# Kept padded buffers and 576-byte rows in the expert choice, and the sampling's preparation by halves of the image

## The chip, the cores and the metric

The kernel runs on one core of a Trainium2 chip. The metric is the time of one launch on the device, in microseconds (us). The core has five engines, each with its own queue of instructions: PE (matrix products; its weight loads are shown as PEld), DVE and ACT (vector and activation work), POOL (here mostly indirect loads, which it issues itself) and SP (which only issues transfers). Transfers are carried out by 16 DMA engines.

## The reference

Four blocks of a network on x of shape (4, 128, 64, 64): in each, x gains a "conv" of its layer norm over channels, and then a "ffn" of the layer norm of its tokens. The kinds differ by layer: involution and a recurrence; deformable sampling and expert choice; a clipped convolution and expert choice; attention and a top-2 mixture. The change lies in layer 0's recurrence, layer 1's sampling and the two expert choices:

```python
# sampling (x has been normalized over channels)
off = conv2d(x, w_off, b_off)                      # 9 taps x (dy, dx)
mask = sigmoid(conv2d(x, w_mod, b_mod))
py = row + ky + dy;  px = column + kx + dx
y0 = floor(py);  x0 = floor(px);  ly = py - y0;  lx = px - x0
# v00 v01 v10 v11: the pixels at (y0 | y0+1, x0 | x0+1), 0 outside the image
sampled = (v00*(1-ly)*(1-lx) + v01*(1-ly)*lx + v10*ly*(1-lx) + v11*ly*lx) * mask
out = einsum('bckhw,ock->bohw', sampled, weight) + bias

# expert choice (x has been normalized over its 128 features), E=64, K=8
probs = softmax(x @ gate_w.T + gate_b, axis=tokens)
topv, topi = top_k(probs per expert, K)
pooled = sum over k of x[topi] * topv              # per image and expert
out = gelu([pooled, 1] @ weight1); out = [out, 1] @ weight2
x[topi] += out * topv
```

## The kernel before

x stays on the chip as `xs`, 128 channels by 4 images of 4096 tokens; a chunk is 512 tokens (8 image rows, CH), so an image has 8 chunks (NCH). The phases run one after the other. The code under `manual_schedule` (ORDERED engines: the sweeps of the recurrence, the sampling's plans and loop, both phases of the expert choice) is issued in program order on every engine and queue; around it, as at the start of the recurrence, a scheduler orders the instructions of a queue. A wait of one instruction holds everything behind it on the same engine. Transfers by nc.sync go out on SP's queue in that order.

**Recurrence** (L452 to L587). It loads W, its transpose `rnn_wt`, V's transpose `rnn_vt` and gamma and beta (L473 to L480), then sums V's transpose up on PE (`rnn_pb`, L514), normalizes the tokens (L181 to L188) and sweeps over the sequence in segments; 1028 to 1236 us in the profile. Whether a further sweep is needed is decided by a flag that is read back.

**Sampling** (`deformable`, L590 on). For every image a table in HBM, `dcn_table`, holds for every (row, column) of a 66 x 66 grid four pixels of 128 channels each, the corners of a square: 2 KB, so that one indirect load fetches what one tap of a token needs. `plan(b)` is the preparation of one image, written as a generator that yields after each small step:

- 16 zero writes for the borders (L667, L669), on SP's queue;
- for the 8 chunks: centring on PE (L686), a copy into the padded image `dcn_pad` (L689, DVE), squares (L694, ACT), then variances on PE (L676), root (L700), reciprocal in four parts (L704) and scaling (L710 on PE, L715 on DVE);
- four times two chunks: 16 transposes on PE (L724), ACT copies into `dcn_xt` (L726), and four writes of 512 KB into the table, one for each corner q, in rows of 512 bytes (L731);
- twice four chunks: the offsets, 72 matmul records (L744), bias (L753), transposes (L757) and copies into `dcn_off` (L762);
- `places`: the indices `dcn_idx` (L772 to L789) and the four corner weights (L796 on).

The offsets' weights and biases, the grids of positions (iota on POOL, L638, and casts on DVE, L640) and the two padded buffers (a memset of the whole on POOL, L247) are set up ahead of plan(0), which runs alone. Then a loop over images, chunks and taps issues gathers on POOL (L816), four to a chunk and tap; ACT (L830) and DVE (L833 to L841) weight the corners, PE (L856, L857) adds and transposes them two steps later, and the convolution follows. Each step (two gathers) also takes one step of the next image's plan. Gathered tiles have 14 buffers, the weighted ones 15 each.

**Expert choice** (L911 on, run for layers 1 and 2). Two images are a pair; 2 images x 64 experts are the 128 rows of `moe_chosen`. Phase A: `stat` sums up squares of a chunk (L1008 to L1018); `scales` and `inverted` give 1/deviation (L1031, L1035); `turn_scales` transposes it (L1041); `logits` multiplies the gate's product by it (L1054 to L1068: rb, the deviations spread over the experts; pl, the product); `largest` finds the 8 largest and their places (L1087 on); `exponentials` the softmax's sum (L1101); `rows` transposes a chunk's tokens (L1076), copies them (L1078) and, on POOL, their scale (L1079) into `moe_xt`, and writes 512 rows of 129 numbers into `moe_table` (L1081); `ask` fetches the chosen rows (L1108); `pool` sums them (L1122 on). `mark` and `choose` (L972, L977) turn the logits into the weights used by the add-back. Phase B loops over 16 groups of four experts, for which 2 MB of weights each come from HBM (L985, L987), and a last part adds the results back to xs.

Of the kernel before, what the change touches and what calls it, by code (L numbers as in the profile page):

```python
# [17 lines left out]
F32 = mybir.dt.float32  # L18
# [222 lines left out]
def padded_pair(net, pool, pad, name):  # L241

    side = H + 2 * pad
    out = []
    for i in range(2):
        t = pool.tile([P, side, side], F32, name=f"{name}{i}", bufs=1)
        net.nc.gpsimd.memset(t, 0.0)  # L247
        out.append(t)
    return out
# [202 lines left out]
def recurrence(net):  # L452
# [16 lines left out]
    with ExitStack() as ctx:  # L469
        sb = ctx.enter_context(tc.tile_pool(name="rnn", bufs=1))  # L470
        yp = ctx.enter_context(tc.tile_pool(name="rnn_y", bufs=3))
# [8 lines left out]
        nc.sync.dma_start(gb[:, 1:2], ins["L0_ffn_beta"])  # L480
        xn = sb.tile([P, LEN, B, SEGS], F32, name="rnn_xn")
# [58 lines left out]

        ps = ctx.enter_context(tc.tile_pool(name="rnn_ps", bufs=2, space=PSUM))
# [44 lines left out]
        with tc.manual_schedule(engines=ORDERED):  # L586
            sweep(0, True, begin())  # L587


def deformable(net):  # L590
# [5 lines left out]

    tc, nc, ins = net.tc, net.nc, net.ins
    KK, PAD = 9, 1  # L600
    SIDE = H + 2
    NO = 3 * KK
    Q4 = 4
    BANKS = {"pt": 3, "out": 2, "pd": 1, "pv": 1}
    GATHERED = 14
    with ExitStack() as ctx:
        dram = ctx.enter_context(tc.tile_pool(name="dcn_dram", bufs=1, space=bass.MemoryType.DRAM))
        tables = [dram.tile([SIDE, SIDE, 4, P], F32, name=f"dcn_table{b}") for b in range(B)]
        one = ctx.enter_context(tc.tile_pool(name="dcn", bufs=1))
        sb = ctx.enter_context(tc.tile_pool(name="dcn_s", bufs=2))  # L610
        ps = ctx.enter_context(tc.tile_pool(name="dcn_ps", bufs=2, space=PSUM))

        woff = one.tile([P, KK, 32], F32, name="dcn_woff")
        nc.vector.memset(woff, 0.0)
        nc.sync.dma_start(woff[:, :, 0 : 2 * KK], ins["L1_conv_w_off"])
        nc.sync.dma_start(woff[:, :, 2 * KK : NO], ins["L1_conv_w_mod"])
        boff = one.tile([P, 1], F32, name="dcn_boff")
        nc.vector.memset(boff, 0.0)
        for q in range(Q4):
            nc.sync.dma_start(boff[32 * q : 32 * q + 2 * KK], ins["L1_conv_b_off"])  # L620
            nc.sync.dma_start(boff[32 * q + 2 * KK : 32 * q + NO], ins["L1_conv_b_mod"])
        wk = one.tile([P, KK, P], F32, name="dcn_wk")
        nc.sync.dma_start(wk, ins["L1_conv_weight"])
        bias = one.tile([P, 1], F32, name="dcn_bias")
        nc.sync.dma_start(bias, ins["L1_conv_bias"])
        zero = one.tile([SIDE, P], F32, name="dcn_zero")
        nc.vector.memset(zero, 0.0)

        grids = []
        for axis in range(2):  # L630
            grid = one.tile([P, NT, KK], I32, name=f"dcn_grid{axis}")
# [8 lines left out]
            nc.vector.tensor_copy(t, grid)  # L640
            grids.append(t)
# [8 lines left out]
        def plan(b):  # L650
# [13 lines left out]
            for q in range(4):  # L664
                dy, dx = divmod(q, 2)
                for r in (H, H + 1) if dy else (0, H + 1):
                    nc.sync.dma_start(tables[b][r, :, q, :], zero)  # L667
                for x in (W, W + 1) if dx else (0, W + 1):
                    nc.sync.dma_start(tables[b][1 - dy : 1 - dy + H, x, q, :], zero[0:H])  # L669

            pv = bank("pv")
            squares = []

            def variances(r):
                for q in range(4):
                    nc.tensor.matmul(  # L676
                        pv[32 * q : 32 * q + 32],
                        net.ewin[:, 31 - r : 63 - r],
                        squares[4 * r + q],
                        start=r == 0,  # L680
                        stop=r == 1,
                    )

            for c in range(NCH):
# [6 lines left out]
                if c == 4:  # L691
                    variances(0)
# [3 lines left out]
            yield  # L696
            variances(1)
            yield
            rstd = sb.tile([P, CH], F32, name="ln_rstd", tag="ln_rstd", bufs=1)
            nc.scalar.activation(rstd, pv, AF.Sqrt, bias=net.eps[1e-6])  # L700
            yield
            for i in range(4):
                part = rstd[:, i * P : (i + 1) * P]
                nc.vector.reciprocal(part, part)  # L704
                yield
            for c in range(NCH):
                rows = slice(32 * (c % 4), 32 * (c % 4) + 32)
                own = 32 * (c % 4) + c // 4
                pb = bank()
                nc.tensor.matmul(  # L710
                    pb, net.ident[rows, own : own + 1].to_broadcast([32, P]), rstd[rows], start=True, stop=True
# [5 lines left out]
            for c2 in range(NCH // 2):  # L717

                xt = sb.tile([W, 2 * ROWS, P], F32, name="dcn_xt", tag="dcn_xt")
                for r0 in range(0, 2 * ROWS, 4):  # L720
# [5 lines left out]
                    nc.scalar.copy(xt[:, r0 : r0 + 4, :], pt)  # L726
# [184 lines left out]
def expert_choice(net, layer):  # L911
# [24 lines left out]
    with ExitStack() as ctx:  # L936
# [54 lines left out]
        with (  # L991
# [147 lines left out]
            for j in range(2):  # L1139
                stat(0, j)  # L1140
# [8 lines left out]
            for j in range(2, 2 * NCH):  # L1149
                stat(0, j)  # L1150
# [822 lines left out]
```

## Time and profile before

| what | us |
|---|---|
| median of 10 runs | 8188.27 |
| lowest to highest | 8182.06 to 8193.77 |
| the profiled execution, its time | 8185.38 |
| its span | 8183.6 |

The mean granted TensorE clock in it was 0.967. The stages, in us from the start of the span:

| stage | from | to |
|---|---|---|
| involution | 0 | 1028 |
| recurrence | 1028 | 1236 |
| sampling, preparation of image 0 | 1236 | 1331 |
| sampling, gather loop | 1331 | 2796 |
| expert choice of layer 1: phase A, phase B, add-back | 2796 | 2930, 3011, 3032 |
| convolution | 3032 | 3352 |
| expert choice of layer 2 | 3352 | 3585 |
| attention and the mixture | 3585 | 8183 |

A profile line of the timeline has the start, the time to the end, the engine, the line of the kernel, the operation with its output and inputs, and in brackets how long the engine had been idle and what ended it. Lines of equal operations that follow each other closely are joined, with their count behind the x. SPq is SP's queue, on which a transfer is issued; the time shown there is that of issuing (a queue that is full makes it longer), not of the transfer.

### The profile page before, as it was taken

Reading aid. Unit: us, or ns where it says so; the run is one execution under the profiler, and the core shown is the slowest. Engines: PE = TensorE matmul, PEld = TensorE weight load, DVE = VectorE, ACT = ScalarE, POOL = GpSimd, SP = SyncE. Lnnn points to the kernel's source line nnn. Section 1 sums busy time; section 2 is a strip of 40 time slices with the busy share of each in tenths; the row PEclk is TensorE's granted clock in tenths of the full one; section 3 lists DMA queues with packets and bytes.
Section 4 is the critical chain, followed back from the end, with each engine's and each line's share of the span. In section 5 each row is a group of like instructions: output and inputs, shape, how many; then the busy total and the mean of one; then the engine's idle time right before and its main releaser. Section 6 shows DMA issues by size and latency. Waiting matters only on the chain.

```text
span 8183.6 us, 144876 instructions
## 1 busy us (share of the span) xinstructions
PE 7547.4 (92%) x59022; PEld 3229.0 (39%) x59022; DVE 5535.6 (68%) x8689; ACT 3769.0 (46%) x7100; POOL 5296.2 (65%) x3019
## 2 busy tenths in 40 slices
PE   8999986777777779879999999999999999999899
PEld 2222243555555434333444344443444334444333
DVE  7888856888888642247776667766777677677155
ACT  4444433444444420313555555555555555555521
POOL 5898904777777410105888788887788777888700
PEclk9999998999999989988999999999999999999999
DMA  6434206877877570232554444544545444455400
GB/s 183 95 75 97 49 2 157 249 220 237 240 217 209 164 214 0 47 145 64 105 111 105 102 106 101 112 105 101 107 102 110 105 101 106 107 105 110 99 22 24
DMA packets 333940, 963.78 MB, mean 118 GB/s; under 512 B 43412, under 2 KB 148948, under 8 KB 275412
## 3 DMA queue, kind: packets, MB, share of 16 engines
q0 software_dynamic: 143872, 673.30, 34.9%
q1 hardware_dynamic: 189396, 281.18, 12.6%
q8 instruction: 464, 7.60, 0.4%
q14 instruction: 208, 1.70, 0.1%
HBM read 468.89 MB, written 82.78 MB: 67 GB/s over the span
## 4 chain that ended last, share of the span: by engine, by line
PE 60%; DVE 11%; DMA 8%; issue 3%; ACT 1%; POOL 1%; SPq 1%; DVEq 0%; POOLq 0%; ACTq 0%
PE att_pv L1576 15%; PE att_sc L1663 13%; PE att_mx L1520 11%; DMA dcn_g<-dcn_table,dcn_idx 6%; PE att_sc L1564 5%; DVE dcn_part L836 3%; PE conv_po L1330 3%; DVE dcn_part L833 3%; PE top_po L1876 3%; DVE dcn_sum L841 2%; DMA moe_w<-in_L_ffn_weight 1%; PE top_pw L1852 1%; DVE att_most L1531 1%; PE moe_pd L1008 1%; SPq L731 1%
## 5 line engine op out<-in xcount | busy, mean ns | idle before, releaser
L1595 POOL TENSOR_TENSOR att_acc<-att_acc,att_ex 128x2048 f32<-128x2048 f32 x640 | 2902.5, 4535 | 637.4 <-ACT att_ex L1664 618.1
L1531 DVE TENSOR_REDUCE att_most<-att_mx 128x2 f32<-128x1024 f32 x2016 | 2462.4, 1222 | 1071.0 <-PE att_mx L1520 991.5
L1664 ACT ACTIVATE att_ex<-att_sc 128x512 f32<-128x512 f32 x4096 | 2223.7, 594 | 1771.2 <-PE att_sc L1663 1488.1
L1663 PE MATMUL att_sc<-att_q,att_k 32*128 32x512 f32 x8192 | 2455.3, 606 | 0.0
L1520 PE MATMUL att_mx<-att_k,att_q 32*128 32x512 f32 x8064 | 2291.8, 647 | 13.0 <-DVE att_parts L1543 10.9
L1564 PE MATMUL att_sc<-att_rows,att_ones_b 32*128 32x256 bf16 (+1 forms) x6144 | 1502.4, 306 | 4.7 <-ACT att_ex L1664 4.7
L816 POOL DMA_INDIRECT dcn_g<-dcn_table,dcn_idx x1152 | 1101.5, 956 | 437.0 <-DMA dcn_g<-dcn_table,dcn_idx 124.0
L1576 PE MATMUL att_pv<-att_ex,att_vals 128*32 128x256 f32 x16384 | 1309.8, 391 | 0.0
L1520 PEld LDWEIGHTS att_mx<-att_k,att_q 32*128 32x128 f32 x8064 | 610.9, 185 | 867.4 <-issue 706.3
L409 POOL TENSOR_TENSOR inv_prod<-inv_seen,inv_prod 128x512 f32<-128x512 f32 (+1 forms) x672 | 837.5, 1274 | 94.1 <-ACT inv_prod L408 94.1
L411 DVE SCALAR_TENSOR_TENSOR inv_prod<-inv_pk,bspan,inv_seen 128x512 f32<-128x512 f32 (+1 forms) x1120 | 774.6, 743 | 140.1 <-PE inv_pk L398 139.8
L1576 PEld LDWEIGHTS att_pv<-att_ex,att_vals 128*32 128x32 f32 x16384 | 322.5, 108 | 1318.9 <-issue 1300.8
L1663 PEld LDWEIGHTS att_sc<-att_q,att_k 32*128 32x128 f32 x8192 | 818.3, 183 | 11.0 <-issue 8.3
L830 ACT ACTIVATE dcn_one<-dcn_g,dcn_w 128x128 f32<-128x128 f32 x1152 | 457.7, 401 | 791.2 <-DMA dcn_g<-dcn_table,dcn_idx 789.6
L857 PE MATMUL dcn_pt<-ident,dcn_sum 128*128 128x128 f32 x2304 | 514.4, 307 | 256.7 <-DVE dcn_sum L841 256.1
L408 ACT ACTIVATE inv_prod<-inv_pk,bspan 128x512 f32<-128x512 f32 (+1 forms) x672 | 436.7, 683 | 503.1 <-PE inv_pk L398 492.0
L856 PE MATMUL dcn_pt<-ident,dcn_one 128*128 128x128 f32 x2304 | 481.1, 292 | 83.9 <-ACT dcn_st L873 71.6
L398 PE MATMUL inv_pk<-inv_red,wtap 32*96 32x512 f32 (+1 forms) x3584 | 511.4, 636 | 7.4 <-DMA inv_seen<-inv_image 7.4
L856 PEld LDWEIGHTS dcn_pt<-ident,dcn_one 128*128 128x128 f32 x2304 | 395.9, 202 | 294.9 <-issue 146.0
L857 PEld LDWEIGHTS dcn_pt<-ident,dcn_sum 128*128 128x128 f32 x2304 | 369.3, 202 | 337.8 <-DVE dcn_sum L841 336.8
L833 DVE TENSOR_SCALAR dcn_part<-dcn_g,dcn_w 128x128 f32<-128x128 f32 x1152 | 405.7, 352 | 124.7 <-DMA dcn_g<-dcn_table,dcn_idx 92.2
L420 PE MATMUL inv_out<-inv_prod,inv_fold 96*32 96x512 f32 (+1 forms) x3584 | 477.9, 605 | 8.5 <-DVE xs L428 8.5
(346 smaller groups left out, 6861.2 us busy)
## 6 DMA issues: line engine op xcount, KB each, us to landing
att_sum<-att_ex POOLq DMA_DIRECT2D x320, 1024.0 KB, 7.5
inv_seen<-inv_image SPq DMA_DIRECT2D x256, 266.0 KB
moe_w<-in_L_ffn_weight SPq DMA_DIRECT2D x64, 1024.0 KB
dcn_table<-dcn_xt SPq DMA_DIRECT2D x64, 512.0 KB
att_sum<-att_ex SPq DMA_DIRECT2D x32, 1024.0 KB
att_sum<-att_acc POOLq DMA_DIRECT2D x32, 1024.0 KB, 7.0
dcn_g<-dcn_table,dcn_idx POOLq DMA_INDIRECT x1152, 3.7
moe_table<-moe_xt SPq DMA_DIRECT2D x64, 258.0 KB
```

Of the source, the lines that this page charges most:

```text
L409: nc.gpsimd.tensor_mul(of, view, of)
L411: nc.vector.scalar_tensor_tensor(out=of, in0=as_shape(pk[0:m], of), scalar=by, in1=view, op0=ALU.add, op1=ALU.mult)
L816: nc.gpsimd.indirect_dma_start(out=g, out_offset=None, in_=rows, in_offset=bass.IndirectOffsetOnAxis(ap=idx[:, j + i, k : k + 1], axis=0),)
L856: nc.tensor.matmul(out, one_, net.ident, start=i == 0, stop=False)
L857: nc.tensor.matmul(out, s, net.ident, start=False, stop=i == 3)
L1520: nc.tensor.matmul(pm[i] if alone else pm[:, i, :], q[r, t * P : (t + 1) * P], ks[r, kc * CH : (kc + 1) * CH], start=True, stop=True,)
L1531: nc.vector.tensor_reduce(most[:, 2 * half : 2 * half + 2, kc], pm, AX.X, ALU.max)
L1564: nc.tensor.matmul(pe[:, cols], ones_b[r], lows[g][r, cols], start=cols.start == 0, stop=False)
L1576: nc.tensor.matmul(block["pv"][r, cols], vals[b][:, t, r], ex[:, h, cols], start=t == 0 and half == 0, stop=t == NT - 1 and half == 1,)
L1595: nc.gpsimd.tensor_add(block["acc"], block["acc"], ex)
L1663: nc.tensor.matmul(pe, ks[r, t * P : (t + 1) * P], qs[c][r], start=False, stop=True)
L1664: nc.scalar.activation(ex[:, h, :], pe, AF.Exp)
```

## The change

Four things are edited.

1. What of the sampling needs no data of the image (weights, biases, grids, the zero tile and the zero writes of all four tables) is made by a class `Sampling`, which the recurrence calls after its own loads. The memsets and casts of it are on POOL.
2. The table is [row, column, dx, dy, channel], so that the two rows of a square that lie one above the other are next to each other; a transposed tile has one row more, copied from the tile before, and is written in pieces of 1 KB, two writes of 1 MB for each pair of chunks in place of four of 512 KB. Zero writes are 6 an image instead of 16.
3. The preparation goes by halves of the image, and the offsets of a half are found as soon as the rows for it are scaled. The padded buffers get zeros at the edges only (this helper is used by the convolution too). The rings `one` and `sum` have 12 and 11 buffers.
4. In the expert choice, a row of the table has 144 numbers (576 bytes) in place of 129; five buffers `moe_xt` are kept, with zeros behind the scale written once; the scale is copied by ACT; the deviations are spread by one matmul with a ready-made selector (`moe_own`, 16 copies on POOL); the gate's product, b1's transposes, the rows, `mark` and `choose` stand elsewhere; the second pair's sum of exponentials is taken in 8 chunks into scratch, and the exponentials are taken again in phase B.

```diff
@@ padded_pair
-        net.nc.gpsimd.memset(t, 0.0)
+        for edge in (t[:, 0:pad], t[:, pad + H :], t[:, :, 0:pad], t[:, :, pad + W :]):
+            net.nc.gpsimd.memset(edge, 0.0)
@@ recurrence
-def recurrence(net):
+def recurrence(net, beside):
...
         nc.sync.dma_start(gb[:, 1:2], ins["L0_ffn_beta"])
+        made = beside()
...
+class Sampling:
+    def __init__(self, net, one, dram):
...
+        self.tables = [dram.tile([SIDE, SIDE, 2, 2, P], F32, name=f"dcn_table{b}") for b in range(B)]
+        zero = one.tile([SIDE, 4 * P], F32, name="dcn_zero")
+        nc.gpsimd.memset(zero, 0.0)
+        self.woff = woff = one.tile([P, KK, 32], F32, name="dcn_woff")
+        nc.gpsimd.memset(woff, 0.0)
         nc.sync.dma_start(woff[:, :, 0 : 2 * KK], ins["L1_conv_w_off"])
...
+        self.wk = one.tile([P, KK, P], F32, name="dcn_wk")
+        nc.sync.dma_start(self.wk, ins["L1_conv_weight"])
...
                 nc.gpsimd.iota(grid[p], pattern=pattern, base=base, channel_multiplier=step)
             t = one.tile([P, NT, KK], F32, name=f"dcn_at{axis}")
-            nc.vector.tensor_copy(t, grid)
+            nc.gpsimd.tensor_copy(t, grid)
...
+        for table in self.tables:
+            for y in (H, H + 1):
+                nc.sync.dma_start(table[y].rearrange("x a b c -> x (a b c)"), zero)
+            for dx in range(2):
+                for x in (W, W + 1) if dx else (0, W + 1):
+                    nc.sync.dma_start(table[0:H, x, dx].rearrange("y b c -> y (b c)"), zero[0:H, 0 : 2 * P])
...
+def recurrence_and_deformable(net):
...
+        deformable(net, recurrence(net, lambda: Sampling(net, one, dram)))
@@ deformable, plan
+            def turned(c2):
+                xt = sb.tile([W, 2 * ROWS + 1, P], F32, name="dcn_xt", tag="dcn_xt")
+                if c2 == 0:
+                    nc.vector.memset(xt[:, 0, :], 0.0)
+                else:
+                    nc.scalar.copy(xt[:, 0, :], xts[-1][:, 2 * ROWS, :])
...
-                    nc.scalar.copy(xt[:, r0 : r0 + 4, :], pt)
+                    nc.scalar.copy(xt[:, r0 + 1 : r0 + 5, :], pt)
...
-                for q in range(4):
-                    dy, dx = divmod(q, 2)
-                    r0 = 2 * ROWS * c2 + 1 - dy
+                pairs = bass.AP(
+                    tensor=xt.tensor, offset=xt.offset, ap=[list(xt.ap[0]), [P, 2 * ROWS], [1, 2 * P]]
+                )
+                r0 = 2 * ROWS * c2
+                for dx in range(2):
                     nc.sync.dma_start(
-                        tables[b][r0 : r0 + 2 * ROWS, 1 - dx : 1 - dx + W, q, :].rearrange("r x c -> x r c"),
-                        xt,
+                        tables[b][r0 : r0 + 2 * ROWS, 1 - dx : 1 - dx + W, dx].rearrange("r x b c -> x r (b c)"),
+                        pairs,
                     )
+                    if c2 == NCH // 2 - 1:
+                        nc.sync.dma_start(tables[b][H, 1 - dx : 1 - dx + W, dx, 0], xt[:, 2 * ROWS, :])
...
+            for h in range(2):
+                squares = []
+                for q in half:
+                    yield from centred(4 * h + q, squares)
+                yield from deviations(squares)
+            yield from inverted(0)
+            for c in half:
+                yield from scaled(c)
+            yield from turned(0)
+            yield from inverted(1)
+            yield from turned(1)
+            for c in half:
+                yield from scaled(4 + c)
+            yield from offsets(0)
+            yield from turned(2)
+            yield from offsets(1)
+            yield from turned(3)
             yield from places(b, off)
...
-                s = sb.tile([P, P], F32, name="dcn_one", tag="one", bufs=15)
+                s = sb.tile([P, P], F32, name="dcn_one", tag="one", bufs=12)
...
-                s = sb.tile([P, P], F32, name="dcn_sum", tag="sum", bufs=15)
+                s = sb.tile([P, P], F32, name="dcn_sum", tag="sum", bufs=11)
@@ expert_choice
-    K, ROW = 8, P + 1
+    K, ROW = 8, P + 16
...
-                for i in range(2):
-                    own = 32 * q + 2 * i + c // 4
...
+                nc.tensor.matmul(pb, own[rows, c // 4, :], rstds[p][rows], start=True, stop=True)
...
+            xts = [sb.tile([P, 4, ROW], F32, name=f"moe_xt{i}", bufs=1) for i in range(5)]
+            for t in xts:
+                nc.gpsimd.memset(t[:, :, P:ROW], 0.0)
...
-                nc.gpsimd.tensor_copy(xt[:, :, P], turned[p][:, i, c, :])
+                nc.scalar.copy(xt[:, :, P], turned[p][:, i, c, :])
...
+                    for c in range(NCH):
+                        sq = sb.tile([P, CH], F32, name="moe_sq", tag="moe_sq", bufs=5)
+                        lg = chosen[p][:, c * CH : (c + 1) * CH]
+                        nc.scalar.activation(sq, lg, AF.Exp, bias=negs[p], accum_out=sums[:, c : c + 1])
+                    nc.vector.tensor_reduce(totals[p], sums, AX.X, ALU.add)
...
-            for j in range(2):
-                stat(0, j)
...
             for j in range(5):
                 stat(1, j)
             turn_scales(0)
+            pg = bank("b", "pg")
+            nc.tensor.matmul(pg[:, 0:E], net.cent, gate, start=True, stop=True)
+            nc.vector.tensor_copy(cgate, pg[:, 0:E])
...
             for j in range(5, 2 * NCH):
                 stat(1, j)
+                if j % 3 == 0:
+                    rows(0, j // 3 - 2)
             scales(1)
-            exponentials(0, neg)
+            exponentials(0)
             inverted(1)
...
+            for c in range(4, NCH):
+                rows(0, c)
+            turn_scales(1)
+            for c in range(NCH):
+                logits(1, c)
+                for n in (2 * c, 2 * c + 1):
+                    rows(1 + n // NCH, n % NCH)
+            largest(1)
+            for c in range(NCH):
+                rows(3, c)
+                ask(0, c)
+            exponentials(1)
             for j in range(K):
                 ask(1, j)
             pool(0)
...
             pool(1)
@@ phase B, in the loop over groups g
+                if g == 2:
+                    mark(0)
                 if g == 4:
+                    choose(0)
+                if g == 5:
+                    nc.scalar.activation(exps, chosen[1], AF.Exp, bias=negs[1])
+                if g == 7:
                     mark(1)
-                if g == 7:
+                if g == 9:
                     choose(1)
```

## The prediction

> **What bounds the kernel now.** I read the busy table, then the windows by stage, the timeline at the stage borders, and the chain of waits. The change touches four places: the start of the recurrence, the sampling from 1236 to 2796, and phase A of both expert choices (2796 to 2930, 3352 to 3485). In the windows the columns are busy us of each engine, granted clock, DMA share, GB/s:
>
> ```profile
> 1236.00:1331.00 95.00, 51.26 (x266) 21.55 (x266) 32.84 (x53) 18.61 (x31) 11.28 (x7) 0.76 0.61 118
> 1331.00:2796.00 1465.00, 1129.08 (x5974) 771.62 (x5974) 1246.97 (x3655) 638.61 (x1530) 1101.46 (x1152) 0.94 0.76 224
> 2796.00:2930.00 134.00, 106.09 (x434) 45.87 (x434) 53.72 (x62) 67.88 (x108) 22.34 (x55) 0.86 0.55 120
> 2930.00:3011.00 81.00, 61.63 (x768) 33.34 (x768) 18.62 (x42) 14.57 (x33) 0.00 (x0) 0.87 0.93 339
> ```
>
> The second stretch is the gather loop. POOL issues 1152 gathers of 0.954 us with 0.307 us between them (354 us idle without the first wait); 1152 x 1.261 = 1453, the length of the loop. So what happens beside the loop is free while POOL is never kept; the preparation of images 1 to 3 is there. The preparation of image 0 is not: POOL stands still for 95 us.
>
> ```profile
> 1236.14 4.04 POOL L638 IOTA dcn_grid<- 64x288 int32 x4 [208.55 <-ACT rnn_y L569]
> 1240.24 7.39 POOL L247 MEMSET dcn_pad<- 128x4356 f32 x2
> 1247.72 1.87 DVE L689 COPY dcn_pad<-dcn_pt 128x512 f32<-128x512 f32 x3
> 1275.28 41.99 SPq L731 DMA_DIRECT2D dcn_table<-dcn_xt  x16
> 1302.57 9.62 PE L744 MATMUL dcn_pv<-dcn_pad,dcn_woff 128*32 128x512 f32 x72
> 1330.39 0.31 DVE L789 CAST dcn_idx<-dcn_row 128x288 int32<-128x288 f32 x1
> 1331.00 1.22 POOL L816 DMA_INDIRECT dcn_g<-dcn_table,dcn_idx  x1 [83.37 <-DMA dcn_table<-dcn_zero]
> ```
>
> The first centred rows wait for the memset (1247.72); no table row leaves before 1275.28; the 16 writes drain one by one (DMA share 0.97 between 1290 and 1317); the offsets stand behind them on PE (1302.57), and the indices, ready at 1330.7, release the first gather. The wait is named after a zero write; the index cast ends as late.
>
> The other two places:
>
> ```profile
> 1027.87 0.43 SPq L477 DMA_DIRECT2D rnn_vt<-in_L_ffn_Vt  x1
> 1030.24 0.49 PE L514 MATMUL rnn_pb<-rnn_vt 128*128 128x128 f32 x2 [1.31 <-DVE xs L428]
> 2801.38 0.66 PE L1142 MATMUL moe_pg<-moe_gate,cent 128*128 128x64 f32 x2 [2.81 <-DMA moe_gate<-in_L_ffn_gate_w]
> 2803.16 6.03 PE L1008 MATMUL moe_pd<-xs,cent 128*128 128x512 f32 x8
> 2810.11 3.70 PE L1008 MATMUL moe_pd<-xs,cent 128*128 128x512 f32 x8
> 2869.73 40.10 SPq L1081 DMA_DIRECT2D moe_table<-moe_xt  x27
> 2916.04 0.97 POOL L1108 DMA_INDIRECT moe_asked<-moe_table,moe_idx  x1 [6.97 <-DVE moe_diag L1122]
> ```
>
> PE's first recurrence matmul has its weight by 1030.24. In the expert choice PE waits for the gate, then runs 8 matmuls at a cold clock (6.03 for 3.70); the row writes go at 40.10 / 27 = 1.49 us a block of 512 rows.
>
> **Price of a descriptor.** A dcn_table write of 1024 rows of 512 B takes 2.9 us in the chain: 64 descriptors on each of 16 engines, 45 ns. A moe_table block has 32 an engine: 46 ns for 516 B. Weight loads in phase B move 2 MB (64 of 2 KB an engine) in 5.42 us: 85 ns. For 1 KB no row exists. Bounds: 45 ns (no dearer than 512 B) and 91 ns (same 181 GB/s). I take the straight line between the rows, 59 ns: 3.8 us for a new 1 MB write, where two old ones took 5.8.
>
> **A. Recurrence start.** Everything of the sampling that needs no data (2 memsets, 4 iotas, 2 casts on POOL; 10 small loads and 24 zero writes on SP) now stands where PE waits for rnn_vt. In the built order four loads (dcn_wk 0.33, w_off 0.67, w_mod 0.71, b_off 0.81 us on SP's queue in the old place, with gaps 2.9) go before rnn_w; the zero writes come after gamma and beta. POOL is free from 1026.97 and its memsets of some 0.9 us hold w_off by 0.5. So rnn_vt goes out near 1031.3, and with the 2.4 us that lay between issue and matmul PE starts near 1033.7 instead of 1030.24: +3.4, plus a few matmuls at the cold clock after a longer idle. I take +4; bounds +1.5 (a landing of 1.4) and +8 (3.4, and 4 for ten cold matmuls as in the 6.03 row). The zero writes, 24 x about 1.1 = 26 us of queue, lie under the 206 us recurrence, and rnn_ends' memsets, behind POOL's preparation, are first needed in its sweeps.
>
> **B. Image 0.** After the recurrence POOL has only 8 edge memsets (1 to 2 us). The first pad copy then waits for PE alone: 1237.8, -9.9. By halves: 4 centrings and squares to 1241; variance matmuls of four, table load 1.28 and root 0.69 while the second half is centred; 4 reciprocals of 0.85 to 1250; 4 scalings on a cold PE to 1254; 16 transposes with copies to 1256.7: first write there, not at 1275.3. It costs a second root and 3.4 us more of reciprocals, which lie under the first two writes. Then the second pair turned by 1260, offsets 0 (8 us) to 1271, third turned to 1276.6, offsets 1 to 1284, fourth turned to 1289.5; places follow the offset copies of 1286.5 by 6.8: indices 1293.3. The last two writes, issued 1289.5, drain by 1297 at 3.8 us each and land some 2 us on: first gather 1299. At 91 ns: 1289.5 + 11.6 + 2.5 = 1303.6; slips in my hand order could reach 1307. I take 1302: -29, bounds -24 and -33. The cover: offsets and places, formerly behind the writes, now set nearly the same end; if the writes were free it would still be 1294.
>
> **C. Gather loop.** Images 1 to 3 keep about 113 preparation steps against 144 available, so they end in time. DVE gains 3.4 us of reciprocals an image with 15% free. The one- and sum-buffers fall from 15 to 12 and 11, about 6 pairs, for a use two pairs later. 0; bounds from the two 80 us stretches in which a table is written: in one POOL's busy time drops from 30.25 to 29.6 in 40 us, 2% or 1.7 us; three tables, -6 to +6.
>
> **D. Expert choice, twice.** The gate product moves behind the deviations: 2803.16 becomes about 2798.7, -4.5, and the cold 2.3 goes; it gives back 0.7 of matmul, and about 1.1 for b1's transposes between the pools. One rb matmul of 128 columns for two of 64: about -0.14 x 8 a pair. Four blocks are turned during the statistics: 4 x 0.51 of PE plus ACT. POOL's scale copy (0.19) goes to ACT, two per logits round, whose ACT-paced 3.03 us becomes some 3.5: +3.8 over 8 rounds. So the second maximum starts between 2895 and 2898 (2895.3 now). Behind it, the marking and choosing (4.41 + 4.42 on DVE) leave the path for phase B, which the weight DMA bounds (share 0.93) with DVE busy 18.6 of 81; one more exponential of 3.7 goes there too. Eight blocks of the last image follow the second maximum's logits; at 1.5 us, asking begins near 2912.5 for 2916.0. But the chunked exponentials hold the first pool until about 2914.5 (2913.9 now), and two pools of 6.1 and b1 in between end at 2928 for 2930.1. I take -2 a layer, -4; bounds -6 (46 ns, maximum at 2895) and +4 (59 ns) a layer.
>
> The Trainium skill ("DMA: Bandwidth & Descriptors", "How a descriptor splits into AXI transactions") speaks against longer rows: a descriptor that starts off a 256 B boundary fetches from the boundary below. Counted that way for the four starts of a 576 B pitch I get 21 beats on average, for 516 B about 20.6. That would be 1.52 us a block; the 45 and 46 ns of this trace (512 B aligned, 516 B not) say alignment is hardly seen, and 1.49. Over 24 blocks the two differ by 0.7 us.
>
> **Sum.** The profiled run took 8185.38 (span 8183.6 and 1.8 around it), 2.9 under the median of 8188.3. +4 - 29 + 0 - 4 = -29, and the conv's edge memsets 0 (its first copy waits for a cold PE, at best -2): in the profiled run 8156, on the median's scale 8159.
>
> **Rivals.** R1, the border is paid twice: small loads delay the recurrence by 8 and writes of 1 KB drain like 512 B ones, 1307: 8188 + 8 - 24 = 8172, no expert gain. For it: no 1 KB row, SP in order. Against: the 85 ns of 2 KB. R2, slower: the 576 B writes are dear. At the 85 ns of a 2 KB row a block takes 2.72 us; 24 blocks from 2867 end at 2932, asking waits for 2935, +19 a layer: 8188 + 4 - 27 + 38 = 8203. It decides from 2.4 us a block, 75 ns. Against: 46 ns at 516 B. R3, the shorter rings or the side work keep POOL: 29.6 busy in 40 us is 1.289 a gather; throughout, 1152 x 0.028 = 32 us: 8191. Against: PE's use is two pairs behind. R4, the halves do not overlap as built (a cold PE, ACT held by a table load): indices near 1315, -16: 8172.
>
> **Numbers.** Forecast 0.68, R1 0.14, R2 0.06, R3 0.06, R4 0.06. Range 8139 to 8182: its low end adds C's and D's gains partly, its high end holds R1 and R4. A change under 0.2% (16 us) can't be told from none: faster is below 8172. All but a sliver of the forecast and half of R1 and R4 make 0.76; slower, most of R2, part of R3 and what I overlooked, 0.09; the rest 0.15.
>
> **What would show it.** First gather about 66 us after the recurrence ends, for 95; 1 MB writes about 3.8 us apart; rnn_pb near 1033.7; 1.26 us a gather still; phase A 132 for 134. I am wrong if the first gather waits beyond 80 us, a gather takes over 1.28, or a block of 576 B rows takes over 2 us.

## The result and the profile after

The changed kernel takes 8143.4 us (median of 8 runs, 8135.9 to 8151.5), before 8188.8 in the runs beside it: a ratio of 0.9944 with a 95% interval of 0.9935 to 0.9953, 45 us less. Its profiled execution took 8146.1 us, span 8144.1, clock 0.968; before 8183.6. The forecast was 8159 within 8139 to 8182. The direction and the range held; 45 us came where 29 were forecast, and the parts below did not come as forecast.

Stage by stage, from the two traces (us; a stage ends where the next one's first matmul, first gather or, for phase B, first load of weights starts):

| stage | before | after | difference | forecast |
|---|---|---|---|---|
| involution, to the end of POOL's last product | 1027.0 | 1028.0 | +1.1 | 0 |
| from there to the sampling's first centring matmul | 209.9 | 217.4 | +7.4 | +4 |
| from there to the first gather | 94.1 | 67.0 | -27.1 | -29 |
| from there to the expert choice | 1465.6 | 1457.1 | -8.5 | 0 |
| its phase A, layer 1, to the pooled rows | 133.3 | 121.9 | -11.4 | -2 |
| phase B, add-back, convolution | 422.2 | 421.2 | -0.9 | 0 |
| phase A, layer 2 | 132.6 | 124.9 | -7.7 | -2 |
| the rest | 4699.0 | 4706.6 | +7.6 | 0 |

The last row has nothing of the change in it. It lay between 4698 and 4710 in the traces of the runs below, so single traces differ there by as much as some of the effects; the small differences above it are read with that in mind.

The row of image 0 needs care as well. Two other traces have the old preparation (those of expert_alone and rings_alone below), and in both the stretch to the first gather is 90.6 us, not 94.1. So some 3.5 of the 27.1 us belong to the one trace of before. What differed is a cast on DVE, ahead of the first copy into the padded image, while POOL fills the two padded buffers. First the trace of before, then that of rings_alone:

```profile
1240.21 7.58 DVE L640 CAST dcn_at<-dcn_grid 128x288 f32<-128x288 int32 x1 [0.88 <-POOL dcn_grid L638]
1240.24 7.39 POOL L247 MEMSET dcn_pad<- 128x4356 f32 x2
```

```profile
1241.04 3.92 DVE L640 CAST dcn_at<-dcn_grid 128x288 f32<-128x288 int32 x1 [0.88 <-POOL dcn_grid L638]
1241.06 7.55 POOL L247 MEMSET dcn_pad<- 128x4356 f32 x2
1244.88 1.87 DVE L689 COPY dcn_pad<-dcn_pt 128x512 f32<-128x512 f32 x3
```

The cast ends 0.16 us after a memset: after the second one in the trace of before, after the first one in the other two. Against the two that agree, the change takes 23.6 us off this stretch.

The timeline of the changed kernel at the recurrence's start and around image 0:

```profile
1029.64 1.68 SPq L611 DMA_DIRECT2D dcn_woff<-in_L_conv_w_mod  x1
1032.92 0.43 SPq L477 DMA_DIRECT2D rnn_vt<-in_L_ffn_Vt  x1
1035.32 0.77 PE L515 MATMUL rnn_pb<-rnn_vt 128*128 128x128 f32 x2 [5.32 <-DMA dcn_boff<-in_L_conv_b_off]
...
1244.63 0.95 POOL L248 MEMSET dcn_pad<- 128x66 f32 x8 [210.20 <-ACT rnn_y L571]
1246.59 1.50 DVE L703 COPY dcn_pad<-dcn_pt 128x512 f32<-128x512 f32 x2 [0.28 <-issue]
1265.05 28.57 SPq L765 DMA_DIRECT2D dcn_table<-dcn_xt  x7
1297.68 0.31 DVE L845 CAST dcn_idx<-dcn_row 128x288 int32<-128x288 f32 x1
1312.40 1.22 POOL L872 DMA_INDIRECT dcn_g<-dcn_table,dcn_idx  x1 [66.82 <-DMA dcn_table<-dcn_xt]
```

The edge memsets are gone in 0.95 us, the first copy follows PE at once, and the first table write leaves 19.7 us after the first centring matmul (1245.40), where before it took 38.4. But the indices are ready at 1298.0 and POOL still waits 14 us: now the writes end last. In a window of that stretch (columns as before, DMA share and GB/s at the end) they run at an even 191 GB/s:

```profile
1270.00:1300.00 30.00, 21.31 (x186) 8.69 (x178) 10.17 (x31) 7.84 (x14) 0.00 (x0) 0.96 0.97 191
```

So a 1 MB write takes 5.5 us, not 3.8. In the expert choice the opposite happened:

```profile
2793.69 0.33 PE L1217 MATMUL moe_pg<-moe_gate,cent 128*128 128x64 f32 x2
2857.90 14.46 SPq L1144 DMA_DIRECT2D moe_table<-moe_xt  x13
2876.61 0.94 POOL L1178 DMA_INDIRECT moe_asked<-moe_table,moe_idx  x1 [11.48 <-DMA moe_table<-moe_xt]
2891.40 0.37 SPq L1042 DMA_DIRECT2D moe_w<-in_L_ffn_weight  x1
```

13 blocks of longer rows are issued in 14.46 us, 1.11 a block, where 516-byte rows took 1.49, and asking begins 107.1 us into the phase instead of 119.4. Both prices had been read from rows of the trace of before, and both were wrong, in opposite directions. The experiments are about that, and about which edit carries which gain.

### The profile page after: what moved, and what is told of

It reads as the page before. It is cut to its first block, busy times and chain, and to the rows that moved or that the text cites. A ratio compares the mean times of both kernels' runs of the same rounds, so it can differ in the third digit from the quotient of the medians.

```text
span 8144.1 us, 144746 instructions
## 1 busy us (share of the span) xinstructions
PE 7543.9 (93%) x58958; PEld 3226.4 (40%) x58958; DVE 5538.3 (68%) x8706; ACT 3787.7 (47%) x7214; POOL 5265.5 (65%) x3014
## 4 chain that ended last, share of the span: by engine, by line
PE 53%; DVE 2%; issue 1%; DMA 1%; ACT 0%; POOL 0%; SPq 0%; POOLq 0%; ACTq 0%; DVEq 0%
PE att_pv L1647 15%; PE att_sc L1734 13%; PE att_mx L1591 11%; PE att_sc L1635 5%; PE top_po L1947 3%; PE top_pw L1923 1%; DVE att_most L1602 1%; DMA moe_w<-in_L_ffn_weight 1%; PE att_sc L1564 0%; PE att_sc L1695 0%; PE top_po L1945 0%; PE att_sc L1678 0%; PE att_mx L1489 0%; PE att_sc L1525 0%; PE top_pd L1884 0%
## 5 line engine op out<-in xcount | busy, mean ns | idle before, releaser
L1734 PEld LDWEIGHTS att_sc<-att_q,att_k 32*128 32x128 f32 x8192 | 819.7, 183 | 10.8 <-issue 8.1
```

The lines of the kernel that those rows point to most:

```text
L1734: nc.tensor.matmul(pe, ks[r, t * P : (t + 1) * P], qs[c][r], start=False, stop=True)
```

## The experiments

The first four ran on another chip, on which before takes 8540.3 us (median of 30) and has a granted clock of 0.932: the gather loop takes some 1805 us there. In the loop PE's granted clock is 0.78 to 0.80 in these four traces, 0.93 to 0.95 in the others, and in the trace of sampling_alone POOL stands for 418 us in pauses of over 0.5 us, mostly for DVE and ACT, against 4 us in that of before. They are compared with before on that chip, and stage by stage with each other; the later seven ran on chips on which before takes 8187.

**The halves of the change.** The changed kernel with the whole function of the expert choice as before, and the kernel before with the changed one. The first of the two against the changed kernel:

```diff
 def expert_choice(net, layer):
...
-    K, ROW = 8, P + 16
+    K, ROW = 8, P + 1
...
-            for j in range(2 * NCH):
+            for j in range(2):
+                stat(0, j)
...
```

> The changed recurrence start, sampling and padded buffers with the expert choice of before. Theory (the gains add up stage by stage): the changed kernel's trace has the first gather 18.6 us earlier than before and the gather loop 8.5 us shorter, so this kernel should be about 27 us under before, near 8161, with both phases A at the 133 us of before and gathers of 946 ns. Rival (the shorter gathers, 946 for 954 ns, have nothing to do with the sampling's edits but with the program around them): the gathers go back to 954 ns here and the gain is about 19.

> The changed expert choice with the recurrence and sampling of before. Theory: phase A of the two layers shrinks by 11.3 and 7.7 us as in the changed kernel's trace, so about 19 us under before, near 8169; the gathers stay at 954 ns. Rival: part of those 19 us comes from the sampling part (what it leaves in the queues at the start of phase A), and this kernel gains under 12.

Measured: sampling alone 8530.9 us, ratio 0.9989 (0.9980 to 0.9999); expert choice alone 8522.5, 0.9978 (0.9968 to 0.9987). By stages: in the first the first gather comes 67.0 us after the first centring matmul and the phases A take 134.1 and 133.3; in the second 90.6 and 122.8 and 123.2. So the gain ahead of the loop goes with the sampling's edits and that of phase A with the expert choice's, whose 18 us (11.3 and 10.1 between the two traces) are as large as in the changed kernel. The first one's total, 9.5 us instead of 27, is smaller than forecast. On this chip its way to the first gather is 23.6 us shorter than in the second, but its recurrence is 4.4 us longer and its loop 6.6 (1811.5 and 1804.9, first gather to last), though its gathers are shorter; here the loop takes 1.57 us a gather and is not paced by POOL's 1.26. The median gather is 946 ns with the sampling's edits and 957 without, so that belongs to the sampling too.

**The row size alone.**

```diff
-    K, ROW = 8, P + 16
+    K, ROW = 8, P + 1
```

> The changed kernel with rows of 129 numbers (516 bytes) again, in the same five kept buffers and the same order. Theory A (the row size matters: 576-byte rows drain in about 1.05 us a block where 516-byte rows take 1.49): the last 8 blocks behind the second maximum take about 3.5 us longer, and asking and pooling with them, so +3.5 a layer, +7 in all over the changed kernel, with the row writes again 1.45 to 1.5 us apart. Theory B (the order alone made the gain): within 2 us of the changed kernel.

Measured: 8522.4 us, ratio 0.9983 (0.9974 to 0.9993). The phases A are 132.0 and 130.0 us, against 122.8 and 123.2 of the kernel with the expert choice alone on the same chip: +9.2 and +6.7. That is more than theory A's 3.5, but not all of it is the row size. The second maximum starts at 99.1 and 96.3 us of the phase here, at 93.8 and 93.3 there, and ahead of it PE was granted less of its clock. In layer 1, first with 516 bytes, then with 576, the windows of some logits rounds and the start of one (the number behind PEld, DVE, ACT and POOL is PE's granted clock):

```profile
3206.00:3218.00 12.00, 12.00 (x30) 4.72 (x28) 1.38 (x2) 4.91 (x12) 0.00 (x0) 0.50 0.34 91
3212.46 0.69 DVE L1116 TENSOR_TENSOR moe_chosen<-moe_chosen,moe_pl 128x512 f32<-128x512 f32 x1 [5.12 <-PE moe_pl L1111]
```

```profile
3223.00:3235.00 12.00, 12.00 (x54) 5.68 (x52) 2.75 (x4) 8.01 (x20) 0.00 (x0) 0.94 0.48 144
3230.22 0.69 DVE L1060 TENSOR_TENSOR moe_chosen<-moe_chosen,moe_pl 128x512 f32<-128x512 f32 x1 [2.42 <-ACT moe_chosen L1059]
```

A round takes 5.81 us at a clock of 0.50 and 3.11 at the better one. The changed kernel, with 576 bytes, has the same slow rounds in some layers: in the second trace of it (changed_again, below) the second maximum starts at 99.2 in layer 1 and at 93.4 in layer 2. So these 5.3 and 3.0 us are no effect of the rows. From the second maximum to the phase's end it is 32.9 and 33.7 us with 516 bytes and 28.9 and 29.9 with 576: +3.9 and +3.7, close to theory A's 3.5 and beyond theory B's 2. The window in which the last blocks drain, first with 516 bytes, then (in the kernel with the expert choice alone) with 576:

```profile
3243.00:3252.00 9.00, 2.28 (x11) 1.88 (x9) 2.52 (x5) 6.11 (x19) 0.00 (x0) 0.50 1.22 186
```

```profile
3255.00:3261.00 6.00, 0.88 (x7) 0.64 (x6) 2.10 (x5) 5.38 (x17) 0.00 (x0) 0.78 1.01 296
```

186 GB/s are 1.42 us for a block of 264 KB (44 ns a descriptor), 296 GB/s are 1.00 us for a block of 295 KB (31 ns): more bytes in less time. With 516-byte rows the new order gains 2.1 and 3.3 us against the 134.1 and 133.3 of the old one on this chip, near the -2 a layer that I forecast, but with the slow rounds in it. Asking starts at 118.3 and 116.3 us there, where 576-byte rows have it at 108.9 and 109.3.

**The queue at the recurrence's start.** The recurrence's loads and `beside()` under an order that includes SP:

```diff
+        with tc.manual_schedule(engines=ORDERED | {ENG.SP}):
...
-        made = beside()
+            made = beside()
```

> The changed kernel with the recurrence's own five loads kept ahead of the sampling's on SP's queue. Theory (the small loads ahead of rnn_vt cost the recurrence's start): PE's first recurrence matmul within 2.5 us of the involution's last addition instead of 5.3, and the recurrence 4 to 8 us shorter: about 5 us under the changed kernel. Rival (the recurrence of the changed kernel is longer by 7.4 us for another reason, such as a cold clock or SP's and POOL's later work beside it): no more than 2 us gained.

> The changed kernel itself, beside before and the next one on one chip, so that the two can be compared without the difference between chips. All theories: 35 to 50 us under before, the first gather 67 us after the sampling's first centring matmul.

> The recurrence's loads ahead of the sampling's, the second time, now beside the changed kernel. Theory (the queue order costs the recurrence's start 4.4 us, as PE's first matmul showed in the first look): 3 to 6 us under the changed kernel, and PE's first recurrence matmul 4 to 5 us earlier. Rival (the start is given back before the recurrence's end, because the sweep waits for other things): less than 2 us.

Measured: on the slower chip 8512.8 (0.9972, 0.9962 to 0.9982). Side by side on the other: the changed kernel 8144.2 (0.9947, 0.9934 to 0.9961), loads first 8138.7 (0.9942, 0.9928 to 0.9955). PE's first recurrence matmul comes at 1031.4 instead of 1035.8:

```profile
1029.50 0.43 SPq L478 DMA_DIRECT2D rnn_vt<-in_L_ffn_Vt  x1
1031.44 0.46 PE L516 MATMUL rnn_pb<-rnn_vt 128*128 128x128 f32 x2 [2.88 <-DMA rnn_vt<-in_L_ffn_Vt]
```

Of these 4.4 us, 2.4 are not the queue's: the involution ends at 1029.0 in the one trace and at 1026.6 in the other. Counted from there the matmul comes after 4.8 us instead of 6.7, and on the slower chip after 4.9 instead of 6.7 and 6.8 (before: 3.3). So the order of the loads is worth 1.9 us at the start, shown on two chips. That they reach the end is not shown: the medians differ by 5.5 us in the right direction, but the intervals overlap, and in the traces of this pair the recurrence's end differs by 0.2 us (1240.4 and 1240.2). A lower clock may hide it there. From that first matmul to the first centring one it took, in the traces with the changed sampling, 204.6 to 205.4 us at a granted clock of 0.97 or 0.98, 208.3 and 208.4 at 0.95, and 208.8 and 210.1 at 0.93; loads first had 0.93, the changed kernel beside it 0.97. So the 3.4 us beyond the start in the table above go with the lower clock of that trace and are no steady property of the change.

**What limits the writes.** 40 writes of zeros to scratch tables during the recurrence, when little else is transferred:

```diff
+        a = wide("probe_a", 64, SIDE, 4, P)
+        for i in range(8):
+            nc.sync.dma_start(
+                a[8 * i : 8 * i + 8, 1 : 1 + W, 0, :].rearrange("r x c -> x r c"),
+                src[0:64].rearrange("p (r c) -> p r c", c=P),
+            )
...
```

> The changed kernel with 40 writes of zeros into scratch tables, while the recurrence leaves the transfers idle, 2 MB of each kind: (a) from 64 partitions 512-byte pieces as in the old corner table, (b) from 64 partitions 1 KB pieces as in the new one, (c) the same from 128 partitions, (d) 1 KB pieces from 64 partitions into a dense table, then from 128 partitions dense rows of (e) 516, (f) 576 and (g) 512 bytes; GATHERED is 12 here to make room. Theory 1 (the number of partitions that are read limits the table writes): a, b and d near 180 to 190 GB/s, c, f and g near 270 or more. Theory 2 (the gaps in the table, pieces that are far from each other in HBM, limit them): a, b and c near 190, d, f, g 270 or more. Theory 3 (16 bytes off a 64-byte boundary is what makes 516 slow): e alone near 180 beside f and g near 270.

One steady window inside each kind, in the order a to g (DMA share and GB/s at the end of the line):

```profile
1053.00:1059.00 6.00, 6.00 (x17) 1.75 (x16) 3.29 (x3) 3.49 (x7) 0.00 (x0) 1.00 0.84 209
1063.00:1070.00 7.00, 7.00 (x34) 1.98 (x32) 4.81 (x6) 5.24 (x11) 0.00 (x0) 1.00 0.92 209
1073.00:1077.00 4.00, 4.00 (x18) 1.32 (x15) 3.59 (x4) 2.63 (x6) 0.00 (x0) 1.00 1.09 385
1081.00:1086.00 5.00, 2.84 (x6) 1.06 (x6) 5.00 (x4) 0.28 (x1) 0.00 (x0) 1.00 0.92 210
1090.00:1094.00 4.00, 2.50 (x7) 0.95 (x6) 4.00 (x6) 0.00 (x0) 0.00 (x0) 1.00 1.23 197
1099.00:1103.00 4.00, 2.75 (x12) 1.00 (x13) 3.63 (x6) 0.00 (x0) 0.00 (x0) 1.00 1.16 301
1105.00:1108.00 3.00, 1.54 (x7) 0.57 (x10) 2.98 (x6) 0.00 (x0) 0.00 (x0) 1.00 1.15 346
```

From 64 partitions it is 209 or 210 GB/s whatever the piece (512 bytes, 1 KB, into a table with gaps or a dense one); the same 1 KB pieces from 128 partitions run at 385. Theory 1 holds and theory 2 falls. From 128 partitions, rows of 516 bytes run at 197, beside 301 for 576 and 346 for 512: theory 3 holds in its numbers. (516 bytes are 4 more than a multiple of 64, not 16, and one such size was tried, so which boundary matters is not shown.) There are two limits, and the old writes of the two stages each met a different one at nearly the same 45 ns.

**Smaller rings alone.**

```diff
-                s = sb.tile([P, P], F32, name="dcn_one", tag="one", bufs=15)
+                s = sb.tile([P, P], F32, name="dcn_one", tag="one", bufs=12)
...
```

(and 11 for `sum`, in the kernel before.)

> The kernel before with only the rings of weighted tiles cut to 12 and 11. Theory (the shorter issue of a gather, 946 for 954 ns, comes from where the tiles lie, and the smaller rings move them): the median gather is 946 here too. Rival (it comes from something else of the sampling's edits): 951 to 957 as before; and if the smaller rings hold POOL, the pause between gathers grows over 0.31 us.

Measured: 8186.9 us in one run; the median gather is 953 ns and the loop, first gather to last, 1451.9 us against 1454.1. In that run the rings neither hold POOL nor make the gathers shorter.

**The old order of the preparation, and 512-byte pieces.** Both in the changed kernel:

```diff
-            yield from inverted(0)
-            for c in half:
-                yield from scaled(c)
...
+            for c2 in range(NCH // 2):
+                yield from turned(c2)
+            for c4 in range(NCH // Q4):
+                yield from offsets(c4)
```

> The changed kernel with the steps of an image's preparation in the old order (all scaled, then all turned, then both offsets), everything else of the change kept. Theory (turning the first rows early and putting the offsets between is worth most of the gain, since the writes drain for 44 us from the first one on): the first write some 5 to 7 us later, offsets behind the last turned pair, the first gather 8 to 14 us later than the 67 us of the changed kernel. Rival (the early constants and the short memset made the gain): within 3 us of 67.

```diff
-                    nc.sync.dma_start(
-                        tables[b][r0 : r0 + 2 * ROWS, 1 - dx : 1 - dx + W, dx].rearrange("r x b c -> x r (b c)"),
-                        pairs,
-                    )
+                    for dy in range(2):
+                        nc.sync.dma_start(
+                            tables[b][r0 : r0 + 2 * ROWS, 1 - dx : 1 - dx + W, dx, dy].rearrange("r x c -> x r c"),
+                            xt[:, dy : dy + 2 * ROWS],
+                        )
```

> The changed kernel with each 1 KB piece of the corner table written as two of 512 bytes again (four writes of 512 KB for a pair of chunks). Theory (64 partitions limit the writes by bytes: 208 and 210 GB/s in the probe): the writes take the same 44 us in all, and the first gather stays within 2 us of 67. Rival (a descriptor has its price, as I forecast: 45 ns for 512 bytes, 59 for 1 KB): the writes take about 46 us against 30, and the first gather comes 5 us later or more.

Measured: the old order 8164.6 us in one run, first gather 81.0 us after the first centring matmul, 14 more than in the changed kernel. The timeline shows the indices last again, behind the second offsets:

```profile
1306.78 7.93 PE L782 MATMUL dcn_pv<-dcn_pad,dcn_woff 128*32 128x512 f32 x72
1323.59 0.31 DVE L841 CAST dcn_idx<-dcn_row 128x288 int32<-128x288 f32 x1
1324.19 1.22 POOL L868 DMA_INDIRECT dcn_g<-dcn_table,dcn_idx  x1 [80.85 <-DVE dcn_idx L841]
```

So of the 23.6 us ahead of the loop the order by halves is worth 14.0, and the early constants, the short memset and the pieces together 9.6. With pieces of 512 bytes (8135.1 us in one run) the first gather comes at 70.4: 3.4 us later, the writes at about 178 GB/s for 190. That lies between the two theories' bounds: a small price of the piece, within the limit of the 64 partitions. This run's total is below that of the changed kernel although its first gather is later; 7 us of that lie in the last row of the stages (4699.7 for 4706.6), so the total of a single run is not read here.

**A version with 128 partitions.** On top of the loads first, the table is written in runs of 128 positions of the padded image, beside each the run one image row below:

```diff
-                xt = sb.tile([W, 2 * ROWS + 1, P], F32, name="dcn_xt", tag="dcn_xt")
+                xt = sb.tile([P, 9, 2, P], F32, name="dcn_xt", tag="dcn_xt")
...
+                        for a in range(2):
+                            nc.tensor.transpose(
+                                pt[0:m, i, a, :], flat[:, g + SIDE * a : g + SIDE * a + m], net.ident
+                            )
...
+                    nc.sync.dma_start(
+                        cells[f : f + P * whole, dx].rearrange("(j p) c -> p j c", p=P),
+                        xt[:, 0:whole].rearrange("p j a c -> p j (a c)"),
+                    )
```

> The recurrence's loads first, and the corner table written from 128 partitions: runs of 128 positions of the padded image are turned, each with the run one image row below beside it, 34 runs an image in pieces of 1 KB as before; borders come with the runs, so 3 zero writes an image remain; the rings of weighted tiles are 11 and 10 to make room. Theory (64 partitions limit the writes to about 190 to 210 GB/s, and image 0's first gather waits for them): writes at 300 GB/s or more, 8.9 MB in under 30 us, the first gather released by the indices about 54 us after the first centring matmul instead of 67, so about 13 us under the kernel with the loads first and 55 under before, near 8125 where before is 8187. Rival (the spread of pieces in HBM or the queue limits them, not the partitions): the writes stay near 200 GB/s and the gain is within 3 us of the kernel with the loads first.

Measured: 8119.3 us, ratio 0.9916 (0.9903 to 0.9930), 67 us under before. The writes run at 344 GB/s:

```profile
1264.00:1273.00 9.00, 8.77 (x72) 2.52 (x74) 2.55 (x4) 0.00 (x0) 0.00 (x0) 1.00 1.04 344
```

and the first gather comes 57.3 us after the first centring matmul: 9.7 us gained of the 13 forecast. The indices are ready at 1294.5, and POOL starts at 1299.0: some 4.5 us are still left behind them. The other stages help too: the loop, first gather to last, is 1441.2 us in this trace, 5 less than in the first trace of the changed kernel.

## Why the prediction was right or wrong

**The total.** It fell into the range, in part by luck: the recurrence lost 3 us more than forecast, the way to the first gather gained 2 less (5 less against the traces that agree), the loop and the two phases A gained 8.5 and 15 more, and the last row, which holds nothing of the change, was 7.6 longer.

**The bound.** That POOL's gathers pace the loop and the way to the first gather is what can be shortened held: the preparation's -29 came as -27.1, of which 3.5 belong to the one trace that the forecast was read from. There the first copy stood behind DVE's own cast, which ended with the second memset; the prediction names the memset alone, and its -9.9 for the first copy starts from this trace's 10.8 us after the first centring matmul, where both others have 7.2. Its inner steps: the first write was put 19.8 us after the first centring matmul and came after 19.7; the indices 56.4, and came after 52.6.

**B, the term that was mis-sized.** "I take the straight line between the rows, 59 ns: 3.8 us for a new 1 MB write." It measured 5.5 (86 ns), near my upper bound of 91 ns; the first gather came at 67.0 where that bound gave 66.7. The step that failed is the reading of "45 ns" as a descriptor's price: those writes left 64 partitions, and the probe shows that this, not the descriptor, held them at 178 to 209 GB/s. The weight loads that I drew the line to use all 128 partitions, and go the other way.

**D, the term that failed.** "The 45 and 46 ns of this trace (512 B aligned, 516 B not) say alignment is hardly seen": they say nothing of the kind, since the first row was held by its 64 partitions and the second by its 516 bytes. A 576-byte block measured 1.00 us where I took 1.49; my bounds (-6 to +4) left out that a longer row could be cheaper. That is worth 3.9 and 3.7 us a layer (on the slower chip), not the whole difference between -2 and the -11.4 and -7.7 that came. The second maximum was forecast at 98.4 to 101.4 us of the phase (98.7 and 96.2 before). It came at 93.5 and 96.4, and in the other traces of the new order near 93.5 where no logits round was slow and up to 99.2 where two were: with PE granted its clock the new order is 5 us and more faster there than I had it. So the -2.1 and -3.3 with 516-byte rows agree with my -2 partly by luck, through their slow rounds. The logits round, put at 3.5 us, took 3.1.

**The skill's rule.** By the rule of the Trainium skill ("DMA: Bandwidth & Descriptors", "How a descriptor splits into AXI transactions") I counted about the same beats for both pitches (21 and, counted again, 20.5), and estimated 1.52 us from it. The runs differ: 44 ns for 516 bytes and 31 for 576 on one chip, so a count of beats alone does not rank these writes.

**A.** The first matmul came 5.1 us later than before, 1.1 of it the involution's end: +4.0 at the start, as taken. Its wait is named after the fourth load, but it ends 2.4 us after rnn_vt's issue, the distance that the prediction used. From the involution's end to the first centring matmul it is 209.9 to 210.7 us in the three traces with the old start and 211.1 to 217.4, on average 213.5, in the seven with the changed one and the loads behind: +3.3 where +4 was forecast, with the clock's part in the spread.

**C.** 0 was forecast and -8.5 came in the first trace. From first to last gather it was -7.7 there and -5.5 in the second; the trace with the loads first has 1452.7 us, and the slower chip a longer loop, 1809 to 1815 for 1805. The median gather is 946 to 949 ns in all ten traces with the changed sampling and 953 to 957 in the three without. 8 ns, times 1152, would be 9 us, but the loops do not follow it, so that the shorter gathers make the gain is not shown. The rings are excluded; the cause stays open.

**The rivals.** R1's premise was true (1 KB pieces drain like smaller ones), but the first gather came at 67.0 where R1 had 70, and the recurrence lost 7.4 in one trace and 3.3 on average, not 8; its "no expert gain" fell. R2, the slower one, had the wrong sign. R3 fell with the rings run. R4 fell: the halves overlapped as built, with the indices 52.6 us after the first centring matmul where R4 had 78.

## What to carry to other kernels

Before a price is taken from a row, ask what held that row: two transfers with the same time per descriptor can be held by different things, and a line drawn between them is worth nothing. Count the partitions that a transfer leaves before its bytes, and try a rounder row: here 576 bytes were cheaper than 516. Before a difference between two traces is put down to an edit, look at the same stage in other traces of the same code, and at its granted clock. When work is put ahead of a phase to hide it, look at what the phase's own first loads then queue behind.

## What the runs showed of the hardware

In the probe, a single run, writes to HBM from 64 partitions ran at 209 or 210 GB/s for 512-byte and 1 KB pieces alike, and from 128 partitions at 385 for 1 KB. Rows of 516 bytes ran at 197 GB/s, of 576 at 301, of 512 at 346. The same kernel took 8187 us on one chip and 8540 on another, with granted clocks of 0.965 to 0.968 and 0.932, and the unchanged gather loop 1454 and 1805 us (in the trace of expert_alone), at a clock of 0.94 and 0.78. A round of logits took 3.11 us where PE's granted clock was 0.94 and 5.81 where it was 0.50. A DVE cast that met POOL's memsets ended 0.16 us after one of them in three traces: after the first in two, with 3.9 us, and after the second in one, with 7.58.
